# ScalarE's slot distances in five rows of 130 values instead of one row of 640: one operand's layout in a graph network kernel

## The chip, the cores and the metric

The kernel runs on one core of a Trainium2 chip. The metric is the device time of one execution in microseconds (us), the median of three runs. An engine is named as in the profile: PE is TensorE, PEld its weight loads, DVE is VectorE, ACT is ScalarE, POOL is GpSimd, SP is SyncE, whose queue issues nearly all DMAs here.

## The reference, cut to what matters

`x` holds 128 graphs of 64 nodes with 128 features; `adj` holds 0/1 adjacency matrices, about one entry in eight set.

```python
f_i = broadcast(part_feats[:, :, None, :]); f_j = broadcast(part_feats[:, None, :, :])
messages = mlp(concat([f_i, f_j]), msg_...)      # relu, layernorm, relu, layernorm, linear
messages = messages * coupling_matrix[..., None]
agg = sum(messages, axis=2)
updated = part_feats + mlp(concat([part_feats, agg]), upd_...)
```

A message whose adjacency entry is 0 is multiplied by 0, so only the edges need computing.

## The kernel before

The graphs are taken in 64 pairs. One pair puts 2 x 64 nodes on the 128 partitions. Each graph has 640 slots for its edges (`CAP = 640`), and the edges of a node lie in consecutive slots. For each pair `p` the program builds two 0/1 matrices of 640 columns: one says which node a slot starts at, the other which node it ends at. The steps around the change:

- `rank`, `place` (once per block of four pairs): a scan on VectorE (L731, tile `rk`) numbers the edges; GpSimd turns this into `mid` and `pos`. `mid` is the sum of the first and last slot of a node, and `deg` is the number of its slots.
- `distance(p)` (L876, ScalarE): tile `d` = |mid - slot| for all 640 slots, with `slot` the odd numbers in half precision; `d` is half precision with two buffers.
- `make_tp(p)` (L882, VectorE): tile `tp` = 1 where `d` < `deg`, else 0: whether a slot belongs to the node of that partition. Half precision in and out, both in SBUF, with `deg` read per partition.
- `tp` is then read three times: GpSimd widens it to 32 bits (L891, tile `i`), TensorE multiplies it with `posall` (L908, tile `mk`), and a DMA transposes it (L1018, tile `oh`). VectorE compares `mk` with the slot numbers (L916, tile `j`).
- DMAs on SP's queue (L898) stack halves of `i` and `j` into tile `s`.

The 160 chunks of 512 slots then go through the message network: TensorE gathers the first layer's rows with `s` (L933, tile `hps`), ScalarE applies bias and relu (L938, `h`), TensorE transposes `h` (L943, `hT`) for VectorE's statistics (L629, `st<-hT`), TensorE multiplies by the second layer (L986, `z`), VectorE or ScalarE applies relu (L613 or L997, `y`), and VectorE takes statistics again (L629, `st<-y`). GpSimd prepares biases (L973, `u`), finishes variances (L646 and L647, `m_v`) from which ScalarE takes a root (L653, `m_sq`), and computes the node update's bias and residual (L1082 and L1083, tile `m`; L1087, tile `xo`) and the next block's `posall` (L776). The update network of a block of four pairs follows its messages, and its result `uo` (L1159) is stored by a DMA on SP's queue.

Every step is put on a list with a time, `at(n, tag, fn, ...)`, where `n` is a chunk number; the table `WHEN` shifts single steps. The list is sorted once, and each engine runs its instructions in that order. In the steady part the whole pattern repeats once per block of four pairs, which holds ten chunks: a block passes in 29.3 us where nothing stalls (the `tp` of one place in it starts at 167.39 us in one block and at 196.74 in the next).

## Time and profile before

| | |
|---|---|
| median of 3 runs | 501.84 us (500.96 to 501.89) |
| the profiled execution | 501.05 us, of which the span from first to last instruction is 499.3 |
| granted TensorE clock | 0.997 |
| busy share of the span | PE 97%, PEld 92%, DVE 94%, ACT 80%, POOL 70% |
| L882 (`tp`) on VectorE | 64 times, 38.1 us in all |
| L876 (`d`) on ScalarE | 64 times, 52.1 us in all |

Rows of the timeline give the start in us, the duration in us, engine, line, operation, tiles and count; a bracket at the end gives the idle time ahead of the instruction and what ended it. Rows of a line give the shortest, median and longest duration in ns. Rows of the windows give the length of the stretch and each engine's busy time in it. Rows of the waits give the total in us, how many times, and the longest.

### The profile page before, as it was taken

The page shows a single profiled execution, that of the slowest core. Times are in us where ns is not written, and L with a number is a line of the kernel's source. Part 1 is how long each engine was busy: PE and PEld are TensorE (multiplying, and loading weights), DVE is VectorE, ACT ScalarE, POOL GpSimd, SP SyncE. Part 2 cuts the span into 40 slices and gives each one's busy share as a digit, 9 for nine tenths or more (in the row PEclk, how much of TensorE's full clock was granted, in tenths as well). Part 3 has the DMA queues.
Part 4 walks back from the last instruction along what each step waited for, and adds up shares of the span by engine and source line. Part 5 has one row for each costly group of instructions (what it writes and reads, how often), then busy time and mean ns, then how long its engine had stood idle before and what let it go on. Part 6 is the DMA issues. An engine that isn't in the chain of part 4 may idle for free.

```text
span 499.3 us, 15949 instructions
## 1 busy us (share of the span) xinstructions
PE 486.1 (97%) x5947; PEld 460.6 (92%) x5947; DVE 468.0 (94%) x1225; ACT 397.1 (80%) x907; POOL 349.1 (70%) x563
## 2 busy tenths in 40 slices
PE   7999999999999999999999999999999999999996
PEld 4889999999999999989999998999989999999995
DVE  7999999999999999999999999999999998989985
ACT  6989978878787887868878786887868779867845
POOL 3275776967949776696877859776696859555771
PEclk9999999999999999999999999999999999999998
DMA  4766838376564756646486673666655458626231
GB/s 122 152 140 152 183 100 162 82 165 153 125 139 98 139 142 150 148 113 142 97 167 142 125 152 90 136 137 147 142 122 135 95 120 163 145 68 154 59 41 47
DMA packets 91474, 63.55 MB, mean 127 GB/s; under 512 B 57473, under 2 KB 75522, under 8 KB 91394
## 3 DMA queue, kind: packets, MB, share of 16 engines
q1 hardware_dynamic: 91106, 62.36, 57.7%
q8 instruction: 49, 0.80, 0.7%
q14 instruction: 31, 0.25, 0.2%
q10 hardware_dynamic: 288, 0.13, 0.1%
HBM read 7.15 MB, written 4.19 MB: 23 GB/s over the span
## 4 chain that ended last, share of the span: by engine, by line


## 5 line engine op out<-in xcount | busy, mean ns | idle before, releaser
L986 PE MATMUL z<-w1c,h 128*128 128x128 f32 x1280 | 190.1, 275 | 0.0
L986 PEld LDWEIGHTS z<-w1c,h 128*128 128x128 f32 x1280 | 172.4, 192 | 4.1 <-DVE uy_st L629 0.2
L938 ACT ACTIVATE h<-hps,b0c 128x512 f32<-128x512 f32 x160 | 108.9, 681 | 35.0 <-PE hps L933 34.5
L629 DVE BATCH_NORM_STATS2 st<-hT 128x6 f32<-128x256 f32 x320 | 122.4, 415 | 6.7 <-PE hT L943 5.1
L629 DVE BATCH_NORM_STATS2 st<-y 128x6 f32<-128x256 f32 x320 | 126.9, 418 | 1.6 <-ACT y L997 1.5
L980 ACT ACTIVATE z<-b1b,m_sd 128x128 f32<-128x128 f32 x320 | 117.3, 368 | 9.4 <-DVE y L613 3.7
L943 PE MATMUL hT<-ident,h 128*128 128x128 f32 x640 | 113.0, 276 | 1.9 <-DVE st L629 1.8
L933 PE MATMUL hps<-s,abl 128*128 128x512 f32 (+3 forms) x256 | 96.9, 381 | 2.6 <-ACT h L938 2.2
L933 PE MATMUL hps<-s,abh 128*128 128x512 f32 (+3 forms) x256 | 89.9, 358 | 0.0
L973 POOL TENSOR_TENSOR u<-b1b,m_sd 128x512 f32<-128x512 f32 x80 | 84.3, 1057 | 7.7 <-ACT m_sd L637 7.7
L943 PEld LDWEIGHTS hT<-ident,h 128*128 128x128 f32 x640 | 75.9, 141 | 6.3 <-issue 3.1
L1029 POOL TENSOR_TENSOR w<-oh,m_q 128x192 f32<-128x192 f16 x126 | 62.0, 513 | 8.8 <-DVE m_q L658 2.5
L916 DVE TENSOR_TENSOR j<-mk,cmpt 128x320 fp32r<-128x320 f32 x124 | 59.2, 477 | 6.3 <-PE mk L908 3.6
L891 POOL CAST i<-tp 128x640 fp32r<-128x640 f16 x58 | 41.7, 719 | 32.1 <-DMA s<-i 30.1
L997 ACT ACTIVATE y<-z 128x512 f32<-128x512 f32 x80 | 47.4, 595 | 17.7 <-PE z L986 17.3
L613 DVE CUSTOM_DVE_ANT_0 y<-z,u 128x512 f32<-128x512 f32 x80 | 54.0, 675 | 3.6 <-PE z L986 3.3
L933 PEld LDWEIGHTS hps<-s,abl 128*128 128x128 f32 x256 | 48.8, 191 | 7.7 <-ACT h L938 3.7
L876 ACT ACTIVATE d<-slot,mid 128x640 f16<-128x640 f16 x64 | 52.1, 818 | 1.7 <-POOL mid L765 1.0
L933 PEld LDWEIGHTS hps<-s,abh 128*128 128x128 f32 x256 | 49.1, 192 | 0.2
L647 POOL TENSOR_TENSOR m_v<-m_v,st 128x20 f32<-128x20 f32 x31 | 7.2, 232 | 58.5 <-DVE st L629 57.3
L1044 PE MATMUL ys<-y,w 128*32 128x128 f32 x1488 | 44.1, 274 | 0.0
L1044 PEld LDWEIGHTS ys<-y,w 128*32 128x32 f32 x1488 | 39.6, 110 | 2.5 <-issue 2.1
(193 smaller groups left out, 890.7 us busy)
## 6 DMA issues: line engine op xcount, KB each, us to landing
s<-i SPq DMA_DIRECT2D x124, 160.0 KB, 3.1
s<-j SPq DMA_DIRECT2D x124, 160.0 KB, 2.9
xn<-in_x_dram SPq DMA_DIRECT2D x15, 256.0 KB, 3.9
out_dram<-uo SPq DMA_DIRECT2D x15, 256.0 KB, 2.5
an<-in_adj_dram SPq DMA_DIRECT2D x16, 128.0 KB, 3.4
oh<-tp SPq DMA_TRANSPOSE x64, 3.2
xn<-in_x_dram SPq DMA_DIRECT2D x2, 128.0 KB, 3.0
out_dram<-uo SPq DMA_DIRECT2D x2, 128.0 KB, 2.0
```

Source lines behind the costliest of these rows:

```text
L613: nc.vector._custom_dve(TENSOR_ADD_SAT, out=o, in0=ps, in1=sb, s0=BIG, s1=0.0)
L629: nc.vector.bn_stats(st, src.rearrange("p t c -> p c t"))
L876: nc.scalar.activation(D[p], slot, AF.Abs, bias=blocks[b]["mid"][:, q:q + 1], scale=-1.0)
L916: nc.vector.tensor_tensor(JR[p][:, c], MK.pop((p, k))[:, 0:HC], cmpt[:, c], op=ALU.is_equal)
L933: nc.tensor.matmul(HP[n][:, c:c + w], lhsT=blocks[g // (2 * PB)]["ab", g // 4 % 2][k][:, g % 4, :], rhs=S[g // 2][:, g % 2, e:e + w], star ...
L938: nc.scalar.activation(H[n], HP.pop(n), AF.Relu, bias=b0c)
L943: nc.tensor.transpose(HT[n][:, t, :], H[n][:, t * P:(t + 1) * P], ident)
L973: nc.gpsimd.tensor_tensor(U[n], bc(W["b1b"], CH), SR[q][:, k:k + CH].unsqueeze(2).to_broadcast([P, CH, C]), op=ALU.mult)
L980: nc.scalar.activation(z_of(n)[:, t, :], W["b1b"], AF.Copy, scale=SR[q][:, k:k + 1])
L986: nc.tensor.matmul(ps[:, t, :], lhsT=H[n][:, t * P:(t + 1) * P], rhs=W["w1c"], start=by_vector(n) and t == 0, stop=True, skip_group_check= ...
L1029: (nc.vector if p == NP - 2 else nc.gpsimd).tensor_tensor(WT[p][:, g], oh, qs, op=ALU.mult)
L1044: nc.tensor.matmul(YS[b][g * N + m * HN:g * N + (m + 1) * HN, k, :], lhsT=w[:, g, m, u, :], rhs=y, start=(u == 0), stop=(u == TH - 1), til ...
```

## The change

Tile `d` is allocated as five rows of 130 values, of which the first 128 of each row are used. ScalarE writes the 640 distances into those 5 x 128 places, and reads `slot` as 5 x 128. VectorE reads `d` as five rows of 128 at a step of 130 and writes `tp`, whose layout stays 640 values in a row; in the built program VectorE's input has the pattern 5 x 128 with row step 130, its output the pattern 640. The number of instructions on each engine and their order are the same in both programs; nothing else differs.

```diff
         def distance(p):
             b, q = divmod(p, PB)
-            D[p] = tpp.tile([P, CAP], F16, name="d", bufs=2)
-            nc.scalar.activation(D[p], slot, AF.Abs, bias=blocks[b]["mid"][:, q:q + 1], scale=-1.0)
+            D[p] = tpp.tile([P, TG, P + 2], F16, name="d", bufs=2)[:, :, 0:P]
+            nc.scalar.activation(D[p], slot.rearrange("p (t e) -> p t e", e=P), AF.Abs, bias=blocks[b]["mid"][:, q:q + 1], scale=-1.0)
 
         def make_tp(p):
 
             b, q = divmod(p, PB)
             tp = tpp.tile([P, CAP], F16, name="tp")
-            nc.vector.tensor_scalar(tp, D.pop(p), blocks[b]["deg"][:, q:q + 1], None,
+            nc.vector.tensor_scalar(tp.rearrange("p (t e) -> p t e", e=P), D.pop(p), blocks[b]["deg"][:, q:q + 1], None,
                                     op0=ALU.is_lt)
             TP[p] = tp
```

## The prediction

> **What bounds the kernel now.** I read the page's busy shares first, then the windows of the steady part, then what TensorE waits for there.

> ```profile
> PE 486.1 (97%) x5947; PEld 460.6 (92%) x5947; DVE 468.0 (94%) x1225; ACT 397.1 (80%) x907; POOL 349.1 (70%) x563
> ...
> 175.00:200.00 25.00, 25.00 (x335) 24.17 (x335) 24.26 (x62) 19.99 (x46) 18.18 (x27) 1.00 0.62 144
> 200.00:225.00 25.00, 24.40 (x327) 23.30 (x326) 24.09 (x61) 19.54 (x44) 20.20 (x32) 1.00 0.59 133
> ```

> TensorE sets the pace. From 175 to 200 us it is busy throughout, and VectorE, at 24.26 of 25, has 0.74 us to spare. From 200 to 225 us TensorE idles 0.60 us. A DVE saving is worth something only in stretches of the second kind. The waits from 100 to 400 us show how many there are:

> ```profile
> PE hps L933 <- ACT h L938: 1.7, 3, 0.7
> PE hT L943 <- DVE st L629: 1.5, 3, 0.7
> ...
> PEld hps L933 <- ACT h L938: 2.2, 3, 0.9
> ```

> There are six stalls in 300 us, three behind VectorE and three behind ScalarE, 3.2 us in all by the matmul rows (a little more by the weight loads). That, with a few stalls outside this stretch, is all that a change on VectorE or GpSimd can win.

> **What the changed instruction does now.** The row of the line, and four windows holding one `tp` each, all of one block:

> ```profile
> L882 DVE TENSOR_SCALAR tp<-d,deg x64: 355/514/1100, 6.9 to 439.3; 128x640 f16<-128x640 f16 x64
> ...
> 167.00:168.00 1.00, 0.38 (x1) 1.00 0.00 0
> 171.00:173.00 2.00, 0.67 (x1) 1.00 0.99 129
> 178.00:179.00 1.00, 0.39 (x1) 1.00 0.98 218
> 183.00:185.00 2.00, 1.04 (x1) 1.00 0.03 9
> ```

> One shape, from 355 to 1100 ns. The four of a block take 0.38, 0.67, 0.39 and 1.04 us, 2.48 in all. What GpSimd does beside the third and the fourth explains it:

> ```profile
> 178.46 0.39 DVE L882 TENSOR_SCALAR tp<-d,deg 128x640 f16<-128x640 f16 x1
> 179.95 0.44 DVE L629 BATCH_NORM_STATS2 st<-y 128x6 f32<-128x256 f32 x1 [0.17 <-ACT y L997]
> 183.80 1.04 DVE L882 TENSOR_SCALAR tp<-d,deg 128x640 f16<-128x640 f16 x1
> 178.91 0.72 POOL L891 CAST i<-tp 128x640 fp32r<-128x640 f16 x1 [2.58 <-DMA s<-i]
> 182.95 1.69 POOL L1087 TENSOR_TENSOR xo<-xn,cu2b 128x512 f32<-128x512 f32 x1
> 184.61 1.12 POOL L973 TENSOR_TENSOR u<-b1b,m_sd 128x512 f32<-128x512 f32 x1
> ```

> ```profile
> L629 DVE BATCH_NORM_STATS2 st<-y x320: 357/419/441, 28.2 to 482.4; 128x6 f32<-128x256 f32 x160
> L613 DVE CUSTOM_DVE_ANT_0 y<-z,u x80: 660/673/692, 26.9 to 479.0; 128x512 f32<-128x512 f32 x80
> L1159 DVE SCALAR_TENSOR_TENSOR uo<-mu,um_q,xo x60: 333/341/352, 113.4 to 493.6; 128x128 f32<-128x128 f32 x60
> L731 DVE TENSOR_TENSOR_SCAN rk<-first,an x16: 671/974/1739, 3.6 to 392.9; 128x256 f16<-128x256 f32 x16
> L973 POOL TENSOR_TENSOR u<-b1b,m_sd x80: 1029/1041/1423, 24.5 to 475.3; 128x512 f32<-128x512 f32 x80
> ```

> 320 statistics on `y` stay within 441 ns; L1159, which also reads a per-partition scalar, within 352. The scan L731, with two tensors from SBUF, spreads from 671 to 1739 like `tp`. [...]

> [...] L1159 needs 341 ns for 128 elements, with a per-partition scalar and one element per cycle: L629 at 256 and L613 at 512 elements differ by 254 ns, 1 ns an element. So about 210 ns are fixed, and 380 alone for `tp` leaves 170 ns for 640 elements, four per ns. Bounds for the new form: at four it stays 380; at two it is 210 + 333 = 543; at one 210 + 667 = 877. [...]

> [...]

> **The change part by part.**

> *ScalarE's write.* Same 64 instructions, 640 values each.

> ```profile
> L876 ACT ACTIVATE d<-slot,mid x64: 812/816/840, 5.9 to 428.6; 128x640 f16<-128x640 f16 x64
> ```

> No row here has a stepped output. The spread of 28 ns bounds an effect from above and below; at +28 on 64 it is 1.8 us of an engine idle 20% of the time, hidden in ScalarE's waits for `hps`. I take 0.

> *VectorE, per block.* First 0.38 to 0.54 (+0.16), second 0.67 to 0.54 (-0.13), third +0.15, fourth -0.50: 2.48 becomes 2.17, a saving of 0.31 us, 3.3 over the kernel (64 x 543 = 34.8 against 38.1). The +0.15 of the third is hidden by the wait of 0.17 for ScalarE's `y` at 179.95, and if that cover is gone, the fourth follows 0.15 late.

> *GpSimd, per block.* It no longer pays the 0.08 behind the fourth.

> *SP.* The DMA queue waits for `uo` (L1159) soon after the second `tp`, and the DMAs behind it feed GpSimd's L891. The first two sum to +0.03, so GpSimd's long run begins up to 0.03 later. It keeps 0.05 of its 0.08.

> *A stall behind VectorE*, at 217.66:

> ```profile
> 214.15 1.02 DVE L882 TENSOR_SCALAR tp<-d,deg 128x640 f16<-128x640 f16 x1
> 217.10 0.41 DVE L629 BATCH_NORM_STATS2 st<-hT 128x6 f32<-128x256 f32 x1
> 217.66 0.63 PE L943 MATMUL hT<-ident,h 128*128 128x128 f32 x4 [0.59 <-DVE st L629]
> 217.64 0.28 POOL L646 TENSOR_SCALAR m_v<-st 128x20 f32<-128x20 f32 x1
> 218.26 0.31 ACT L653 ACTIVATE m_sq<-m_v,eps_c 128x20 f32<-128x20 f32 x1 [1.35 <-POOL m_v L647]
> 219.44 0.69 ACT L938 ACTIVATE h<-hps,b0c 128x512 f32<-128x512 f32 x1
> 220.48 0.42 PE L933 MATMUL hps<-s,abl 128*128 128x384 f32 x1
> ```

> VectorE runs without a gap from the fourth `tp` to the statistics that TensorE waits for, so 1.02 - 0.54 = 0.48 us reach the stall. What is late next is ScalarE: its `h` ends at 220.13, and TensorE's next gather, at 220.48, needs it. That chain starts at GpSimd's L646, not at VectorE, and leaves 0.30 (the next fence has 0.05 between `h` and the gather). So 0.30 of 0.48 counts, and with GpSimd's 0.05, 0.35. Three such stalls: -1.05.

> *A stall behind ScalarE*, at 279.93, has the same chain and no room:

> ```profile
> 277.39 0.28 POOL L646 TENSOR_SCALAR m_v<-st 128x20 f32<-128x20 f32 x1
> 279.19 0.69 ACT L938 ACTIVATE h<-hps,b0c 128x512 f32<-128x512 f32 x1
> 279.93 0.44 PE L933 MATMUL hps<-s,abl 128*128 128x384 f32 x1 [0.52 <-ACT h L938]
> ```

> GpSimd is behind its own work here, so only its 0.05 counts. Three stalls: -0.15.

> *The start.* Here VectorE feeds TensorE directly:

> ```profile
> 6.94 0.71 DVE L882 TENSOR_SCALAR tp<-d,deg 128x640 f16<-128x640 f16 x1
> 7.70 0.30 PE L908 MATMUL mk<-tp,posall 128*128 128x320 f16 x1 [1.21 <-DVE tp L882]
> 10.73 0.38 DVE L882 TENSOR_SCALAR tp<-d,deg 128x640 f16<-128x640 f16 x1
> 12.59 0.31 PE L908 MATMUL mk<-tp,posall 128*128 128x320 f16 x1 [0.19 <-DVE s L1353]
> ```

> The first `tp` gets 0.17 shorter, the next two 0.19 (from 355) and 0.16 longer, so the wait at 12.59 ends about 0.2 later: +0.2.

> *Sum:* -1.05 - 0.15 + 0.2 = -1.0. The profiled execution took 501.05 (span 499.3 and 1.75 around it), 0.8 under the median, and would come to 500.05. From the median I get 501.84 - 1.0 = **500.8 us**.

> **The rivals.**

> *All of VectorE's saving counts.* If GpSimd's lateness has its root in VectorE too, by way of the DMAs that its L891 waits for (2.58 us at 178.91), each of six stalls gives up 0.48: 501.84 - 2.9 = 498.9. For it speaks that GpSimd, SP and VectorE wait for each other in a circle; against it, that L646 follows on GpSimd's own work.

> *The wait is only passed on.* ScalarE's `h` takes the place of VectorE's statistics in each stall and the start costs its 0.2: about 501.8. For it speaks that three of six stalls are of that kind already; against it the 0.30 in hand.

> *Slower: the third `tp` reaches TensorE.* It gains 0.15 in each of 16 blocks. This decides from the point where VectorE's wait at 179.95 is under 0.15 rather than 0.17. Then the relu behind it, and in turn TensorE, are late in each block: 16 x 0.15 + 0.2 = +2.6, 504.4. For it: VectorE has only 0.74 us in 25 spare. Against it: the fourth gives 0.50 back 5 us later.

> *One element per cycle.* At 877 ns the third costs +0.49 with 0.17 of cover, so 16 x 0.32 = +5.1: 507. [...]

> *The change does nothing,* if the engine treats five rows like one: 501.8, with `tp` still from 355 to 1100.

> **How the numbers follow.** A measurement of this kernel can tell 0.2%, 1.0 us, from no change. Forecast 0.44, with a range of its own from 500.0 to 501.7: since it lies on that bound, 0.24 of it counts as faster and 0.20 as same. All of the saving: 0.20, faster. Passed on: 0.14, same. Third `tp` late: 0.14, slower. One per cycle: 0.05, slower. Nothing: 0.03, same. So faster 0.44, same 0.37, slower 0.19. The range reaches down to the first rival's 498.9 and up to 503.0, which leaves out most of the slower cases.

> **What would show it.** `tp` between about 535 and 565 ns in all 64, whatever GpSimd does; ScalarE's L876 at 816; L973 not over 1.1 us behind a `tp`. TensorE's waits for VectorE's statistics from 100 to 400 us well under 1.5 us, those for `h` about as they are. The forecast is wrong if `tp` still spreads, if it lies at 380 or 877, if waits for `h` grow by what the others lose, or if TensorE waits in blocks that had none.

## The result, and the profile after

| | before | the change |
|---|---|---|
| median | 501.33 us (22 runs, 498.78 to 504.58) | 498.69 us (22 runs, 497.27 to 500.23) |
| ratio, 95% interval | | 0.9947 (0.9934 to 0.9961): 2.65 us faster |
| the profiled execution | 501.05 us, span 499.3 | 499.65 us, span 497.9, granted clock 0.997 |
| forecast | | 500.8 us, range 498.9 to 503.0, -1.0 us |

The change is faster, by more than twice the forecast, and the time lies 0.2 us below the range. The page of the change, its groups of the lines that the prediction speaks of, its steady windows and TensorE's waits from 100 to 400 us:

```profile
PE 486.0 (98%) x5947; PEld 461.3 (93%) x5947; DVE 465.2 (93%) x1225; ACT 397.3 (80%) x907; POOL 348.4 (70%) x563
```
```profile
L882 DVE TENSOR_SCALAR tp<-d,deg x64: 517/536/547, 6.9 to 437.2; 128x640 f16<-128x640 f16 x64
...
L876 ACT ACTIVATE d<-slot,mid x64: 812/817/839, 5.9 to 426.4; 128x640 f16<-128x640 f16 x64
...
L973 POOL TENSOR_TENSOR u<-b1b,m_sd x80: 1030/1042/1429, 24.7 to 472.8; 128x512 f32<-128x512 f32 x80
```
```profile
175.00:200.00 25.00, 25.00 (x337) 24.21 (x336) 24.26 (x62) 20.38 (x45) 18.24 (x28) 1.00 0.62 143
200.00:225.00 25.00, 25.00 (x336) 24.27 (x334) 24.18 (x63) 20.50 (x46) 21.24 (x33) 1.00 0.65 142
```
```profile
PE hps L933 <- ACT h L938: 1.8, 4, 0.6
PE hT L943 <- DVE st L629: 0.2, 1, 0.2
```

All 64 `tp` now take 517 to 547 ns. ScalarE's writes into stepped rows cost nothing (817 against 816). In these two profiles TensorE's waits for VectorE's statistics fell from 1.5 us to 0.2, its waits for `h` stayed (1.7 and 1.8), and the window from 200 to 225 us, where it had idled 0.60, is full. The fourth `tp` of the block that the prediction showed no longer waits for GpSimd, and L973 behind it takes its usual time. Timeline of the change, VectorE and then GpSimd:

```profile
181.94 1.03 DVE L731 TENSOR_TENSOR_SCAN rk<-first,an 128x256 f16<-128x256 f32 x1
...
183.23 0.52 DVE L882 TENSOR_SCALAR tp<-d,deg 128x640 f16<-128x640 f16 x1
```
```profile
181.14 1.29 POOL L1083 TENSOR_TENSOR m<-m,ub0r 128x512 f32<-128x512 f32 x1
182.38 1.70 POOL L1087 TENSOR_TENSOR xo<-xn,cu2b 128x512 f32<-128x512 f32 x1
184.03 1.04 POOL L973 TENSOR_TENSOR u<-b1b,m_sd 128x512 f32<-128x512 f32 x1
```

0.52 us inside the 1.70 of L1087, where it stood 1.04 before. The scan L731 still meets GpSimd: it ends at 182.97, 0.54 after L1083.

**Where the time came from.** One `tp` stands at the same place of every block, so the starts of two such instructions measure a stretch of the program. Timeline of VectorE before, then of the change; the last row of each is the last computation:

```profile
108.12 0.38 DVE L882 TENSOR_SCALAR tp<-d,deg 128x640 f16<-128x640 f16 x1
...
196.74 0.37 DVE L882 TENSOR_SCALAR tp<-d,deg 128x640 f16<-128x640 f16 x1
...
227.09 0.38 DVE L882 TENSOR_SCALAR tp<-d,deg 128x640 f16<-128x640 f16 x1
...
377.27 0.38 DVE L882 TENSOR_SCALAR tp<-d,deg 128x640 f16<-128x640 f16 x1
...
495.22 0.61 DVE L1159 SCALAR_TENSOR_TENSOR uo<-z,um_q,xo 128x128 f32<-128x128 f32 x2
```
```profile
107.77 0.54 DVE L882 TENSOR_SCALAR tp<-d,deg 128x640 f16<-128x640 f16 x1
...
196.18 0.53 DVE L882 TENSOR_SCALAR tp<-d,deg 128x640 f16<-128x640 f16 x1
...
225.44 0.53 DVE L882 TENSOR_SCALAR tp<-d,deg 128x640 f16<-128x640 f16 x1
...
374.94 0.53 DVE L882 TENSOR_SCALAR tp<-d,deg 128x640 f16<-128x640 f16 x1
...
492.78 0.61 DVE L1159 SCALAR_TENSOR_TENSOR uo<-z,um_q,xo 128x128 f32<-128x128 f32 x2
```

- To 108 us: -0.35.
- The next nine blocks: 269.15 us became 267.17, -1.98.
- From there to the end of the last `uo`: 118.56 became 118.45, -0.11.

That is 2.44 us of work saved, close to the 2.65 between the medians. The spans differ by only 1.4, because the last store's landing happened to be quick in the execution profiled before: 3.5 us from the last `uo` to the end of the span, against 4.5 in the change (the median of the last two stores' landing was 2.0 us there and 3.4 here, and 2.7, 3.3 and 3.4 in the profiles of three more kernels with one row). The two profiled totals alone understate the gain.

Two profiles are a narrow base. Here are the same stretches in the profiles of four kernels with one row and of three with five rows, which differ among themselves only in where the tiles behind `d` lie ("Is it the place in memory?" below):

| | to the `tp` at 108 us | nine blocks | from there to the end of the last `uo` |
|---|---|---|---|
| one row, 4 profiles | 107.81 to 108.12, mean 107.95 | 267.55 to 270.01, mean 269.04 | 118.54 to 118.73, mean 118.63 |
| five rows, 3 profiles | 107.13 to 107.77, mean 107.36 | 267.04 to 267.87, mean 267.36 | 118.35 to 118.45, mean 118.40 |
| difference of the means | -0.59 | -1.68 | -0.23 |

That is -2.50 in all. The nine blocks differ so much within a kind that the two kinds overlap.

**What a stall costs.** A block without one passes in 29.26 us (196.18 to 225.44 in the change). Before, the same block took 30.35 (196.74 to 227.09), 1.09 more, and it holds one stall, the one at 217.66 for which the waits list 0.59 us. Over nine blocks, by the start of the same `tp` in each, what lies above 29.26 adds up so:

| blocks holding | before | the change |
|---|---|---|
| a stall for VectorE's statistics | 3 blocks, 2.84 us | 1 block, 0.92 us |
| a stall for ScalarE's `h` | 3 blocks, 2.72 us | 4 blocks, 2.91 us |
| none listed | 3 blocks, 0.25 us | 4 blocks, 0.00 us |

So in these two profiles two stalls behind VectorE vanished. It was not the shorter `tp` alone that removed them, because something else differs in these blocks: GpSimd's L891, which waits for a stacking DMA. Timeline of L891 and of the scan in the block with the stall at 217.66, before and then in the change; the third pair of rows is the block of the change that kept a stall behind VectorE (it starts at 285.46):

```profile
209.27 0.72 POOL L891 CAST i<-tp 128x640 fp32r<-128x640 f16 x1 [3.59 <-DMA s<-i]
...
212.22 1.68 DVE L731 TENSOR_TENSOR_SCAN rk<-first,an 128x256 f16<-128x256 f32 x1
```
```profile
207.56 0.72 POOL L891 CAST i<-tp 128x640 fp32r<-128x640 f16 x1 [2.34 <-DMA s<-i]
...
211.13 1.06 DVE L731 TENSOR_TENSOR_SCAN rk<-first,an 128x256 f16<-128x256 f32 x1
```
```profile
298.15 0.72 POOL L891 CAST i<-tp 128x640 fp32r<-128x640 f16 x1 [3.65 <-DMA s<-i]
...
301.01 1.77 DVE L731 TENSOR_TENSOR_SCAN rk<-first,an 128x256 f16<-128x256 f32 x1
```

Counted from the start of the block's first `tp`, L891 starts at 209.27 - 196.74 = 12.53 us before, and in the change at 207.56 - 196.18 = 11.38 in the same block and at 298.15 - 285.46 = 12.69 in the later one. GpSimd's work behind L891 moves along with it, and so does the scan that waits for L1083. The kernel before also has blocks in which L891 is on time (11.45 to 11.52), and they hold no stall behind VectorE.

The timelines of thirteen kernels agree on this. Where L891 starts by 11.52, a block takes 29.26 us or at most 0.12 more. Where it starts later, the block is too long by that start less a fixed number. The number depends on the fourth `tp`, and on whether the scan waits for L1083 or has run ahead of it and takes its 0.66 to 0.69 us:

| the fourth `tp` | late blocks in which the scan waits | late blocks in which the scan runs ahead |
|---|---|---|
| one row of 640, 8 profiles | start less 11.40 to 11.45, mean 11.43 (22 blocks) | start less 11.57 to 11.73, mean 11.64 (16 blocks) |
| five rows, 5 profiles | start less 11.74 to 11.81, mean 11.79 (15 blocks) | start less 11.67 to 11.76, mean 11.71 (10 blocks) |

(The eight are the kernel before and seven kernels below: four rows, the two with pairs numbered wrongly, the third alone unshifted, and the three with a longer tile. The five are the change, its two other row steps, the fourth alone, and the two that meet GpSimd. The first of the nine blocks is left out: it is 0.55 to 0.74 us too long in all thirteen, with L891 on time.)

So, at the same lateness of L891, five rows make a late block 0.36 us shorter where the scan waits, and 0.07 where it runs ahead. How late L891 comes is another matter. Its starts beyond 11.42, summed over the eight blocks of a profile, make 3.85 to 6.21 us in the eight profiles and 3.95 to 5.97 in the five. They were 5.51 before and 4.42 in the change, so part of what this pair of profiles shows is the execution and not the change. That the change makes L891 less late is not shown.

### The profile page after: what moved, and what is told of

Read it like the earlier page. It is cut to its first block, busy times and chain, and to the rows that moved or that the text cites. A ratio compares the mean times of both kernels' runs of the same rounds, so it can differ in the third digit from the quotient of the medians.

```text
span 497.9 us, 15949 instructions
## 1 busy us (share of the span) xinstructions
PE 486.0 (98%) x5947; PEld 461.3 (93%) x5947; DVE 465.2 (93%) x1225; ACT 397.3 (80%) x907; POOL 348.4 (70%) x563
## 5 line engine op out<-in xcount | busy, mean ns | idle before, releaser
L938 ACT ACTIVATE h<-hps,b0c 128x512 f32<-128x512 f32 x160 | 109.0, 682 | 36.0 <-PE hps L933 35.5
L629 DVE BATCH_NORM_STATS2 st<-hT 128x6 f32<-128x256 f32 x320 | 122.9, 417 | 7.1 <-PE hT L943 4.8
L629 DVE BATCH_NORM_STATS2 st<-y 128x6 f32<-128x256 f32 x320 | 127.1, 419 | 0.5 <-ACT y L997 0.3
L943 PE MATMUL hT<-ident,h 128*128 128x128 f32 x640 | 112.9, 276 | 0.3 <-DVE st L629 0.2
L933 PE MATMUL hps<-s,abl 128*128 128x512 f32 (+3 forms) x256 | 96.6, 380 | 2.6 <-ACT h L938 2.1
L933 PE MATMUL hps<-s,abh 128*128 128x512 f32 (+3 forms) x256 | 89.8, 358 | 0.0
L973 POOL TENSOR_TENSOR u<-b1b,m_sd 128x512 f32<-128x512 f32 x80 | 83.7, 1049 | 7.6 <-ACT m_sd L637 7.6
L943 PEld LDWEIGHTS hT<-ident,h 128*128 128x128 f32 x640 | 76.3, 141 | 3.4 <-issue 1.2
L1029 POOL TENSOR_TENSOR w<-oh,m_q 128x192 f32<-128x192 f16 x126 | 62.1, 514 | 9.4 <-DVE m_q L658 3.1
L891 POOL CAST i<-tp 128x640 fp32r<-128x640 f16 x58 | 41.8, 720 | 29.3 <-DMA s<-i 27.7
L997 ACT ACTIVATE y<-z 128x512 f32<-128x512 f32 x80 | 47.4, 595 | 17.8 <-PE z L986 17.5
L613 DVE CUSTOM_DVE_ANT_0 y<-z,u 128x512 f32<-128x512 f32 x80 | 54.1, 676 | 4.0 <-PE z L986 3.7
L933 PEld LDWEIGHTS hps<-s,abl 128*128 128x128 f32 x256 | 48.8, 191 | 8.0 <-ACT h L938 3.7
L876 ACT ACTIVATE d<-slot,mid 128x640 f16<-128x640 f16 x64 | 52.1, 818 | 1.7 <-POOL mid L765 1.0
L647 POOL TENSOR_TENSOR m_v<-m_v,st 128x20 f32<-128x20 f32 x31 | 7.3, 234 | 60.9 <-DVE st L629 59.6
L933 PEld LDWEIGHTS hps<-s,abh 128*128 128x128 f32 x256 | 49.1, 192 | 0.2
```

Source lines behind the costliest of these rows:

```text
L613: nc.vector._custom_dve(TENSOR_ADD_SAT, out=o, in0=ps, in1=sb, s0=BIG, s1=0.0)
L629: nc.vector.bn_stats(st, src.rearrange("p t c -> p c t"))
L876: nc.scalar.activation(D[p], slot.rearrange("p (t e) -> p t e", e=P), AF.Abs, bias=blocks[b]["mid"][:, q:q + 1], scale=-1.0)
L933: nc.tensor.matmul(HP[n][:, c:c + w], lhsT=blocks[g // (2 * PB)]["ab", g // 4 % 2][k][:, g % 4, :], rhs=S[g // 2][:, g % 2, e:e + w], star ...
L938: nc.scalar.activation(H[n], HP.pop(n), AF.Relu, bias=b0c)
L943: nc.tensor.transpose(HT[n][:, t, :], H[n][:, t * P:(t + 1) * P], ident)
```

## Experiments

Ratios are to the kernel before, in runs on the same chip, with 95% intervals. "First" to "fourth" are the four `tp` of a block by time, as in the prediction. Their pairs are p%4 = 2, 3, 1 and 0. None of the added memsets touches data that anything reads.

### Is it the pattern? Four rows in place of five

```diff
-            D[p] = tpp.tile([P, TG, P + 2], F16, name="d", bufs=2)[:, :, 0:P]
+            D[p] = tpp.tile([P, 4, 162], F16, name="d", bufs=2)[:, :, 0:160]
```
with ScalarE and VectorE reading and writing 4 x 160. The question is what makes `tp` steady at 517 to 547 ns: the step between the rows, or the shape of five rows of 128. If it is the shape, `tp` should spread from about 360 to 1100 ns again here, and the time be that of the kernel before.

> The changed kernel with tile d in four rows of 160 values at a step of 162 in place of five rows of 128 at 130: ScalarE's output and VectorE's input are stepped as in the change, but both outermost counts (4 and 640) are even. [...] Theory B, the gaps between the rows do it, whatever their number: tp at 536 ns throughout, time ratio to before 0.995 as for the change.

Ratio 0.9964 (0.995 to 0.9977), 500.33 us. The group of `tp` in this kernel:

```profile
L882 DVE TENSOR_SCALAR tp<-d,deg x64: 356/550/1102, 6.9 to 438.0; 128x640 f16<-128x640 f16 x64
```

Rows at a step alone do not make `tp` steady: with four rows it runs in 356 ns at the shortest and takes up to 1102, as in the kernel before (355 to 1100), and with five rows neither. Among five rows the step makes no difference: at 130, 134 and 144 the 64 `tp` take 517, 517 and 516 ns at the shortest and 547 at the longest. Four rows of 160 differ from five of 128 in number and in length; which of the two counts, and why, no run shows. That this kernel is still 0.36% faster than before, with the spread of `tp` kept, was not foreseen, and no run explains it in full (see placement, below). Its late blocks cost as much as those of the kernel before (start less 11.44 where the scan waits).

### Which of the four counts?

These kernels keep one row of 640 for the pairs that `alone` names and use five rows for the others:

```diff
+        def alone(p):
+            return p % 4 != 0 or p < 8
```

This form gives five rows to the fourth alone; the others differ in the last line.

> The changed kernel, but five rows of 130 only for the pairs whose tp met GpSimd in the profile before (the odd ones, and 0, 8, 10, 12, 16); the other 27 keep one row of 640. Theory A (only the tp behind a GpSimd instruction matters, and the third tp's extra 0.15 us is hidden): same time as the change within 0.1%, ratio to before about 0.995; the 27 take 376 to 390 ns and wait for nothing. Theory B (the extra 0.16 us of the first and third tp costs something in each block): 1 to 2 us faster than the change, ratio 0.991 to 0.993. Theory C (the short ones now meet GpSimd, because the steps around them have moved): some of the 27 over 600 ns and a ratio nearer to 1.

> The changed kernel, but five rows of 130 only for the fourth tp of each block (pairs 5, 9, 13 and so on, 15 in all); the other 49 keep one row of 640. Theory A (the fourth tp makes the gain): ratio to before 0.995 or a little less. Theory B (the second tp, before uo and SP's queue, has a share): ratio about 0.997. Theory C (the start, with the first tp, has a share): ratio 0.997 with the first 40 us as in the kernel before.

Both went astray: their pairs were numbered wrongly. The first gave five rows to the second and third `tp` (and some at the start) and not to the fourth, the other to the third alone. They gave 0.9967 (0.9953 to 0.9981) and 0.9958 (0.9941 to 0.9975). Aimed anew by the timeline, with `d` at a place that keeps the tiles behind it on the same multiple of 128 bytes:

> Five rows (at a step of 134, so that the tiles behind d keep their place modulo 128 bytes) only for the tp with remainder 0 by four from pair 8 on, the fourth of each block by time; all others in one row of 640. Theory A: nearly the whole gain, ratio to before 0.995 to 0.997. Theory B (the second tp, ahead of uo and SP's queue, and the start have the larger share): 0.998 or more.

> Five rows (at a step of 134) for every tp that met GpSimd in the profile before: the second and fourth of each block by time, and 0, 5, 9, 10, 13, 17 near the start; the others in one row of 640, at 376 to 390 ns. Theory A (the third tp's extra 0.16 us is hidden): as the change, ratio 0.995. Theory D (VectorE, with 0.31 us less work in each block than in the changed kernel, has more slack to take up late DMAs): 0.993 or less, the fastest of all.

> Five rows only for the third tp of each block by time (remainder 1 by four), as in the run called fourth_only, but at a step of 134, by which the tiles behind d move up by 128 bytes and not by 64. Theory P (that run's 0.996 was the placement): ratio 0.999 to 1.001 here. Theory M (something in the third tp itself helps): ratio 0.996 again.

The fourth alone: 0.9972 (0.9957 to 0.9988). The second and the fourth (and six at the start): 0.9951 (0.9931 to 0.9972), as much as the change. The third alone: 0.9977 (0.9962 to 0.9992). TensorE's waits from 100 to 400 us with the fourth alone:

```profile
PE hT L951 <- DVE st L629: 0.4, 1, 0.4
PE hps L941 <- ACT h L946: 0.3, 1, 0.3
```

In its profile the fourth alone takes away most of the waits for statistics, 1.1 us, and it gives about half of the gain of the medians. (The waits for `h` are 0.3 there against 1.7 before, but a single profile does not tell these apart: the four kernels with one row have 1.7, 1.1, 1.1 and 1.6, the three with five rows 1.8, 1.9 and 1.0.) Its start is that of the kernel before: it reaches the `tp` at 108 us at 107.85. Giving five rows to the two that meet GpSimd, and leaving the first and third in one row (from 361 ns), adds nothing that can be measured over the change (498.47 us, against 498.69 with other runs of before beside it). What the second adds by itself no run shows.

The third alone meets no GpSimd work in the steady blocks and gets 0.16 us longer there, and yet both kernels with it came out faster, by 0.2 and 0.4%. One part of this lies at the start, where the same pairs do meet GpSimd: the `tp` that starts at 24.64 and takes 1.10 us before takes 0.54 in both, and they reach the `tp` at 108 us at 107.16 and 107.22, against 107.81 to 108.12 with one row. The rest stays open.

### Does it count when VectorE is late, and where?

Each of these kernels adds a memset of 485 ns on VectorE in 14 or 15 of the 16 blocks: behind the third `tp` of the change, behind its fourth, and behind the fourth of the kernel before.

```diff
             TP[p] = tp
+            if p % 4 == 0 and p > 4:      # p % 4 == 1: behind the third
+                late = tpp.tile([P, 512], F16, name="late", bufs=1)
+                nc.vector.memset(late, 1.0)
```

> The changed kernel with a VectorE memset of 512 half-precision values (about 0.49 us, touching nothing else) behind the fourth tp of each block, so that VectorE is as late there as before while GpSimd is still never held up. Theory A (VectorE's lateness behind the fourth tp is the whole effect): the gain is lost, ratio to before 0.999 to 1.002, and the waits of TensorE for the statistics of hT come back (about 1.5 us from 100 to 400 us). Theory B (what counts is that GpSimd is no longer held up): the gain stays, ratio 0.995. Theory C (the working of the prediction: 1.05 us of it by VectorE): ratio about 0.997.

(This expectation calls the third `tp` the fourth, by the numbering mistake told above.)

> As the run with the memset before, but in the right place. On VectorE the pairs' tp do not stand in the order of their numbers: the third tp of a block by time is the pair with remainder 1 by four, the fourth the one with remainder 0, so the earlier memset stood behind the third. Here the changed kernel gets the memset of about 0.49 us behind the fourth. Theory A (VectorE's lateness behind the fourth tp is what the gain comes from): the gain is lost, ratio to before 0.999 to 1.001, TensorE waits 1.3 us or more for the statistics of hT from 100 to 400 us. Theory B (GpSimd no longer held up is what it comes from): the gain stays, ratio 0.995. Theory C (half and half): 0.997.

> The kernel before with the memset of 0.49 us behind the fourth tp of each block. Theory A: slower by about as much again as the change is faster, ratio 1.004 to 1.008, more stalls for the statistics of hT. Theory B (GpSimd): no change, ratio 1.000.

| 485 ns added behind | ratio | what it costs |
|---|---|---|
| the third, in the change | 0.9954 (0.9937 to 0.9971) | nothing that can be told |
| the fourth, in the change | 0.9994 (0.9974 to 1.0013) | the whole gain |
| the fourth, in the kernel before | 1.0093 (1.0066 to 1.0119) | 4.7 us more than before |

TensorE's waits from 100 to 400 us in the second and in the third kernel:

```profile
PE hT L946 <- DVE st L629: 1.2, 3, 0.5
PE hps L936 <- ACT h L941: 1.0, 4, 0.3
```
```profile
PE hT L946 <- DVE st L629: 6.2, 6, 1.4
```

VectorE's lateness behind the fourth `tp` is what TensorE waits for, and the later VectorE already is, the more a further delay costs: 6.8 us of memsets (14 x 485 ns) cost about 2.4 in the change and 4.7 in the kernel before. The late blocks say the same. With the memset behind the fourth of the change, those in which the scan waits are too long by L891's start less 11.45 and 11.46 (two blocks), as in the kernel before. In the kernel before the memset makes this 10.88 to 10.97 (five blocks), and even the two blocks with L891 on time become 0.48 and 0.55 us longer. Behind the third the same 485 ns vanish, and the timeline shows where, with the third `tp` of the change ahead of the rows of this kernel:

```profile
177.97 0.55 DVE L882 TENSOR_SCALAR tp<-d,deg 128x640 f16<-128x640 f16 x1
```
```profile
178.29 0.55 DVE L882 TENSOR_SCALAR tp<-d,deg 128x640 f16<-128x640 f16 x1
178.89 0.48 DVE L886 MEMSET late<- 128x512 f16 x1
...
182.58 0.72 DVE L731 TENSOR_TENSOR_SCAN rk<-first,an 128x256 f16<-128x256 f32 x1
...
183.55 0.54 DVE L882 TENSOR_SCALAR tp<-d,deg 128x640 f16<-128x640 f16 x1
```

The scan starts later and takes 0.72 us instead of 1.03. From the start of the third `tp` to that of the fourth it is 183.55 - 178.29 = 5.26 us, and in the change without the memset 183.23 - 177.97 = 5.26 too. The scan waits for GpSimd's L1083 either way, and what comes late ahead of it in such a block loses nothing. At the start the memset is not hidden: this kernel reaches the `tp` at 108 us at 108.12, like the kernel before.

### Does it count when GpSimd is late?

```diff
             TP[p] = tp
+            if p % 4 == 0 and p > 4:
+                late = tpp.tile([P, P], F16, name="late", bufs=1)
+                nc.gpsimd.memset(late, 1.0)
```

> The changed kernel with a GpSimd memset of about 0.2 us (touching nothing else) just ahead of L646 in each block from the third on, in the chain that ends in ScalarE's root. Theory A (GpSimd's chain is the next limit, as the prediction's working has it): the stalls behind ScalarE's h grow by about 0.2 us each and appear in more blocks: ratio to before 0.997 to 0.999. Theory B (GpSimd's chain has room in most executions): ratio 0.995, as for the change.

0.9961 (0.9946 to 0.9975), 499.6 us. The memset took 205 ns, 2.9 us in 14 blocks. The point lies 0.7 us above the change's ratio, and the intervals overlap, so by the medians between nothing and some 1.4 us of the 2.9 was passed on. TensorE's listed waits for `h` did not grow in the one profile (1.3 us, 3 times, against 1.8, 4 times). The blocks of that profile decide more. Its three blocks with L891 on time take 29.26 us, as without the memset. Its late ones are too long by L891's start less 11.52 to 11.56 where the scan waits (three blocks) and less 11.50 and 11.56 where it runs ahead (two), against 11.79 and 11.71 in the mean without the memset. So in a late block GpSimd's lateness counted nearly in full, some 0.15 to 0.27 us for 0.205, and in a block on time not at all.

### Is it the place in memory?

Five rows of 130 make `d` 20 bytes a buffer longer, so the tiles behind it move (by 64 bytes in the built program), among them those that the stacking DMAs read and write. Three kernels keep one row of 640 and only lengthen the tile; two keep the change at other row steps. In the expectations theory P gives the place a share of the gain; in theory M the steady `tp` alone makes it, wherever the tiles lie.

```diff
-            D[p] = tpp.tile([P, CAP], F16, name="d", bufs=2)
+            D[p] = tpp.tile([P, CAP + 10], F16, name="d", bufs=2)[:, 0:CAP]     # also + 30, + 80
```
```diff
-            D[p] = tpp.tile([P, TG, P + 2], F16, name="d", bufs=2)[:, :, 0:P]
+            D[p] = tpp.tile([P, TG, P + 6], F16, name="d", bufs=2)[:, :, 0:P]   # also P + 16
```

> The kernel before, with tile d allocated 20 bytes longer and used as before (one row of 640). Nothing but addresses changes: all tiles behind d move up by 64 bytes, as they do in the changed kernel, so that i, j and s, between which the stacking DMAs copy, begin at a multiple of 128 bytes instead of 64 beyond one. Theory P (part of the gain is this placement): ratio to before 0.996, as in the run with four rows; the DMA packets of 2560 bytes take 166 ns on average as there, and not 174 as before; tp spreads from 355 to 1100 ns as before. Theory M (VectorE's mode alone, the run with four rows being an accident): ratio 1.000, packets 174 ns.

> The kernel before, with tile d allocated 60 bytes longer and used as before: all tiles behind it move up by 128 bytes, so i, j and s lie 64 bytes beyond a multiple of 128 as before. Theory P: no change, ratio 1.000 within 0.15%, packets 174 ns; this also shows what the measurement makes of two kernels that should be equal. If any move of the tiles helps (or a later kernel of a call is always measured faster): ratio about 0.996.

> The kernel before with tile d allocated 160 bytes longer and used as before: the tiles behind d move up by 320 bytes, and i, j and s begin at multiples of 512 bytes. Theory P (placement at a multiple of 128 shortens the stacking DMAs and has a share of its own): packets of 2560 bytes at 166 to 168 ns, ratio 0.997 to 0.999. Theory M: 1.000 even if the packets are shorter.

> The changed kernel with rows at a step of 134 values instead of 130, by which the tiles behind d move up by 128 bytes instead of 64: i, j and s begin 64 bytes beyond a multiple of 128, as in the kernel before. VectorE's instruction is the changed one. Theory P (placement and mode each have a share): packets 174 ns, tp 536 ns throughout, and a ratio of 0.998 (the 1.0 us of the prediction's sum). Theory M: ratio 0.995, as for the change.

> The changed kernel with rows at a step of 144 values, by which i, j and s begin at multiples of 512 bytes. Theory P with 128 bytes as what counts: packets 166 ns and ratio 0.995, as for the change. If larger alignments count too: packets well under 166 ns and a ratio of 0.993 or less. Theory M: 0.995 with packets as they were.

| kernel | ratio | mean time of the stacking DMAs' packets |
|---|---|---|
| before | 1 | 174 ns |
| one row, moved by 64 bytes | 0.9989 (0.9972 to 1.0005) | 167 ns |
| one row, moved by 128 bytes | 0.9999 (0.9986 to 1.0012) | 171 ns |
| one row, moved to multiples of 512 | 0.9984 (0.9971 to 0.9996) | 167 ns |
| the change (moved by 64 bytes) | 0.9947 (0.9934 to 0.9961) | 166 ns |
| five rows, moved by 128 bytes | 0.9949 (0.9931 to 0.9968) | 171 ns |
| five rows, moved to multiples of 512 | 0.9952 (0.9935 to 0.9969) | 168 ns |

The packet times are worked out from the traces: the mean over the packets of more than 1,300 bytes on SP's queue, one profile each. The packets are shorter at the other places (166 to 171 ns against 174), but by itself the place measures 0.1 to 0.2% at most (the intervals reach 0.3%), and nothing beside the five rows: all three placements of the change give the same. So it is the pattern, not the place. It can be a part of what the four-row kernel and one of those with the third alone gained, not all of it.

### What bounds it now? A third buffer for `i`

GpSimd's L891 waits for the stacking DMAs to leave one of the two buffers of `i`. The page's group before, then in the change (busy time and mean, then idle time ahead and what ended it):

```profile
L891 POOL CAST i<-tp 128x640 fp32r<-128x640 f16 x58 | 41.7, 719 | 32.1 <-DMA s<-i 30.1
```
```profile
L891 POOL CAST i<-tp 128x640 fp32r<-128x640 f16 x58 | 41.8, 720 | 29.3 <-DMA s<-i 27.7
```

The wait is 30.1 us before and 27.7 in the change. A third buffer needs memory. The first try took it from `oh` (three buffers instead of four):

```diff
-            IR[p] = tpp.tile([P, CAP], F32R, name="i32", bufs=2)
+            IR[p] = tpp.tile([P, CAP], F32R, name="i32", bufs=3)
-            OH[p] = wp.tile([P, TG, P], F16, name="oh", bufs=4)
+            OH[p] = wp.tile([P, TG, P], F16, name="oh", bufs=3)
```

> The changed kernel with three buffers for tile i in place of two (and three in place of four for oh, to make room), so that GpSimd's L891 doesn't wait for the stacking DMAs two pairs back. Theory A (the stalls behind ScalarE's h start at L891's wait for these DMAs): L891's waits for DMA, 27.7 us in the changed kernel, mostly gone, the stalls for h from 100 to 400 us (1.8 us) mostly gone, ratio to before 0.990 to 0.992. Theory B (the chain starts elsewhere): ratio 0.995, with the wait moved to another instruction. The third buffer of oh less can cost something: then a new wait at L1018 or L1029 shows it.

Ratio 1.0604 (1.0585 to 1.0623), 531.81 us. SP's waits and VectorE's in this kernel:

```profile
SPq L1018 <- POOL usdb L1141: 49.6, 8, 8.3
...
DVE j L916 <- DMA s<-j: 23.0, 7, 4.2
```

The transposing DMA L1018 now holds up SP's queue for a buffer of `oh`, and the stacking of `j` behind it comes late. The fourth buffer of `oh` was needed, and the time of this kernel says nothing on `i`. The second try takes the room from two small constants that only the branch for dense graphs uses, which does not run on this input; there the bias is added by ScalarE instead of by a second product. The third is the same with five rows only for the `tp` that meet GpSimd (the second and fourth, and six at the start).

```diff
-    b0r = row(mb0, "b0r")
-    ones_row = const.tile([1, P], F32, name="ones_row")
+            IR[p] = tpp.tile([P, CAP], F32R, name="i32", bufs=3)
-        nc.tensor.matmul(ps[:, 0:N], lhsT=b0r, rhs=ones_row[:, 0:N], start=False, stop=True)
+        nc.scalar.activation(aT, ps[:, 0:N], AF.Identity, bias=b0c)
```

> The changed kernel with three buffers for tile i in place of two. The room comes from two constants that only the dense fallback uses (a bias row and a row of ones, with the load and the memset that fill them), which takes the bias from the bias column instead; the fallback doesn't run on these inputs. Theory A (the stalls for h start at L891's wait for DMAs): that wait of 27.7 us is gone, the stalls for h from 100 to 400 us mostly gone, ratio to before 0.990 to 0.993. Theory B (they start at other work): ratio 0.995. Theory C (an earlier L891 moves GpSimd's long run so that the scan or the relu of VectorE waits for it more, or SP's queue is upset): 0.997 or more.

> The same third buffer for i with five rows only for the tp that met GpSimd in the profile before (second and fourth of each block by time, and six near the start). Theory A: 0.989 to 0.992, the fastest. If the earlier GpSimd now meets the tp that were alone: some of these over 600 ns, and not faster than the run with five rows throughout.

Ratios 0.9848 (0.9824 to 0.9872), 494.52 us, and 0.987 (0.9846 to 0.9894), 495.97 us. In the first of them GpSimd's group, VectorE's scan, and the `tp` that bound nine blocks:

```profile
L889 POOL CAST i<-tp 128x640 fp32r<-128x640 f16 x58 | 41.6, 717 | 1.7 <-DVE tp L880 1.6
```
```profile
L729 DVE TENSOR_TENSOR_SCAN rk<-first,an x16: 670/903/940, 3.5 to 386.5; 128x256 f16<-128x256 f32 x16
```
```profile
107.12 0.54 DVE L880 TENSOR_SCALAR tp<-d,deg 128x640 f16<-128x640 f16 x1
...
370.64 0.54 DVE L880 TENSOR_SCALAR tp<-d,deg 128x640 f16<-128x640 f16 x1
```

GpSimd no longer waits for the DMAs, TensorE has no listed wait from 100 to 400 us, and nine blocks pass in 263.52 us, 29.28 each, the pace of a block without a stall. The stalls that the change had left, behind `h` too, have their root in the two buffers of `i`. This kernel is faster than the one before and, by the ratios, than the change, and the gain is larger than the 0.990 to 0.993 that was expected. The third kernel lets the third `tp` be fast again, and now that one meets GpSimd:

```profile
L888 DVE TENSOR_SCALAR tp<-d,deg x64: 358/530/1483, 6.9 to 433.2; 128x640 f16<-128x640 f16 x64
```

Its interval overlaps the other's, so the runs do not say which is better. What a third buffer would give with one row of 640 was not tried.

## Why the prediction was right or wrong

**Right: what `tp` costs.** 543 ns was forecast and 536 measured (517 to 547), whatever GpSimd does. The saving on VectorE is 38.1 - 34.3 = 3.8 us against 3.3, since the mean of the 64 is 535 where 543 stood. The rivals "one element per cycle" and "the change does nothing" are out. But the choice of the middle pace, two elements per ns, was the author's guess: no run ahead of the result shows it. Nor does any show the 333 and 667 ns for 640 elements, which need 1.04 ns an element; the rows of L629 and L613 give 254 ns for 256, 0.99, and how long a cycle of VectorE lasts no trace says. With 0.99 the middle value is 210 + 318 = 528. The runs show 536, which beyond the estimated 210 leaves 326 ns for 640 elements, 1.96 per ns.

**Right: ScalarE's write is free, GpSimd's 0.08 comes back** (817 ns; L973 behind the fourth in 1.04).

**Right, for one more reason than given: the third's longer `tp` is hidden.** The wait of 0.17 for `y` did cover it (it is gone in the change). Behind it lies a second cover that the prediction did not see, the scan that waits for GpSimd: even 0.485 more is lost in it in the steady blocks. The rival "slower: the third `tp` reaches TensorE" was priced without that cover, and is out.

**Right: what a stall gets shorter by, 0.35 and 0.05.** At the same lateness of L891 a late block in which the scan waits gets 0.36 us shorter, and one in which it runs ahead 0.07. The first are the stalls behind VectorE and most of the second those behind `h`. The four profiles with one row hold three of the first and two of the second on average, so by themselves these terms come to 3 x 0.36 + 2 x 0.07 = 1.2 us, the 1.05 + 0.15 of the forecast. The rivals "the wait is only passed on" and "all of VectorE's saving counts" are out by this, for they need 0 and 0.48 in each stall. That the 498.9 of the latter came out nearly right is luck, though one thing it named is there: GpSimd's lateness comes from the DMAs that L891 waits for.

**Wrong: "GpSimd is behind its own work", and six stalls of fixed size.** The prediction traced each stall back to L646, which follows on GpSimd's own work, and stopped there. This work began late because L891 waited for a DMA (3.59 us at 209.27, where a block on time has 2.58). Two things failed by it:

- The listed waits, 3.2 us, were taken as all that can be won in the steady part. The nine blocks before were 5.8 us longer than nine without a stall, and the third buffer for `i`, which takes away L891's wait, won 5.6 of them together with the five rows (269.15 against 263.52).
- The six stalls of one profile were taken as fixed. Which blocks are late changes from execution to execution. In this pair of profiles the blocks with stalls changed by -1.92 + 0.19 = -1.73 where the sum has -1.2, with L891 less late in the second. The blocks without a stall gained 0.25 (0.14 in the means over placements), which the sum has at nothing; no run shows why.

**Wrong: "the start", +0.2.** This term had the wrong sign, and it is the largest single part of the miss: the change stands 0.35 us ahead by 108 us, and 0.59 in the means. The wait that the term names is there, about as large as forecast:

```profile
12.74 0.31 PE L908 MATMUL mk<-tp,posall 128*128 128x320 f16 x1 [0.35 <-DVE s L1353]
```

It is 0.35 for 0.19, and it ends 0.15 later. But the term stopped at the third `tp` of the program. A later one in the start met GpSimd, and TensorE waited behind it; timeline before, then of the change:

```profile
24.64 1.10 DVE L882 TENSOR_SCALAR tp<-d,deg 128x640 f16<-128x640 f16 x1
...
26.75 0.63 PE L943 MATMUL hT<-ident,h 128*128 128x128 f32 x4 [0.34 <-DVE st L629]
```
```profile
24.84 0.54 DVE L882 TENSOR_SCALAR tp<-d,deg 128x640 f16<-128x640 f16 x1
...
26.46 0.60 PE L943 MATMUL hT<-ident,h 128*128 128x128 f32 x4
```

The change comes to that `tp` 0.20 late and to the transpose 0.29 early, and stands 0.35 ahead by 108 us. The kernels above bear it out: the two with the third alone have five rows at this `tp` and gain at the start, the fourth alone does not and gains nothing there.

**The sum by terms** (profiled work): blocks behind VectorE -1.92 (forecast -1.05), blocks behind `h` +0.19 (-0.15), the other blocks -0.25 (0), to 108 us -0.35 (+0.2), the rest -0.11 (0): -2.44 against -1.0. By the means over placements it is -1.68 for the nine blocks (-1.2), -0.59 to 108 us (+0.2) and -0.23 for the rest (0): -2.50. No run shows why the rest gained.

**And the base.** The forecast was taken from 501.84, the median of three runs, and 22 runs gave 501.33; 0.5 of the 2.1 us between 500.8 and 498.69 is this. A single profile counts a number of stalls that changes from run to run. With the old `tp` in one row, the profile of before lists 1.5 us of waits for the statistics from 100 to 400 us, and those of the three kernels with a longer tile 3.0, 1.2 and 2.1. With five rows throughout at three placements it is 0.2, 0.2 and 0.7. The mean difference is 1.6, and what one profile showed was 1.3.

## What to carry to other kernels

Here a half-precision VectorE instruction that stood still until GpSimd was done was made slower and steady: five rows of 128 in place of 640 cost it 0.16 us alone (0.38 to 0.54) and saved 0.5 where the two met (1.04 to 0.52). Price a stall by the period of the blocks that hold it against a block without, not by the wait that is listed for it (1.09 us against 0.59 here). Then look for what sets its size, here how late one DMA lets GpSimd start, and compare blocks of the same lateness: two profiles alone made one `tp` look worth 0.95 us a stall where it was worth 0.36. Ask of every lateness what absorbs it behind: in a steady block the same 485 ns cost nothing ahead of a scan that waits anyway, and the whole gain behind it. When a change removes one engine's stalls and leaves another's, follow those to their root: one more buffer for `i` gave another 1.0%.

## What was not expected of the hardware

- With four rows at a step `tp` spreads as with one (356 to 1102 ns against 355 to 1100); with five rows it does not (517 to 547 ns).
- The scan with two tensors in SBUF waits for GpSimd as `tp` did. It spread from 671 to 1739 ns before, and with GpSimd's work elsewhere in time (the third buffer of `i`) from 670 to 940. In the change it ended 0.54 us after L1083 in the block shown. Why the scan and `tp` in one row wait, and the statistics on `y` (357 to 441 ns before) do not, no run shows.
- Moving the stacking DMAs' tiles by 64 bytes or to multiples of 512 changed the mean time of their packets from 174 to about 167 ns, and the kernel's time by 0.2% at most (0.3% by the intervals).
- How late the stacking DMAs let L891 start differs from execution to execution of kernels with the same `tp` (3.85 to 6.21 us in eight blocks), and the time of nine blocks moves with it, by up to 2.5 us between the four kernels with one row. The kernel with four rows was 0.36% faster than the one before and the runs leave the cause open, so a difference of that size should not be put down to a mechanism by its size alone.
